# Slot tiles of a routed layer: probabilities folded into the rows, one operation for ReLU and sum, two of three tiles transposed by DMA, gathers five tiles ahead

## The chip, the core and the metric

The kernel runs on one core of one Trainium2 chip. The metric is device time in microseconds (us), the median of several executions. The core has five engines with their own instruction queues: TensorE (PE in the profile), VectorE (DVE), ScalarE (ACT), GpSimd (POOL) and SyncE (SP). SP here only issues DMAs; POOL also issues the indirect ones.

## The reference, cut to what matters

Two layers run over 4096 tokens of 512 features. The first (attention to a context, then a quantised feed-forward net) and the attention of the second lie before everything that is changed here. The change is in the last part, a net of eight experts that takes the best expert for each token:

```
probs = softmax(x @ Wg + bg)
idx   = argmax(probs)
p     = probs[idx]
e     = idx % 8
out   = relu(x @ We[e] + be[e]) * p      # for the token's own expert only
x     = x + out                          # x in the product is the layer norm of x
```

Here `x` in the products is the normalised row, `x` in the last line the row itself.

## The kernel before

**Tiles.** Tokens lie in 32 tiles of 128 rows. For the experts they are sorted by expert into 39 slot tiles, each of which holds rows of one expert. This sorting is done twice. The first, `routing(True)`, runs along with the attention of tiles 24 to 28 and fills slot tiles 0 to 14 (`NJA = 15`) from the first 22 tiles. The second, `routing(False)`, is cut into steps that stand between `expert(5)` and `expert(11)` and fills slot tiles 15 to 38. Its last steps build one-hot tables on DVE (L1134), and PE multiplies them (32 short matmuls, L1142) to find out which row goes where. DVE then turns the product into row numbers (L1144 to L1148).

**A row in memory.** For each tile `gated` (L996 to L1009) writes to `x_dram` rows of 516 numbers: the 512 of x, the mean, the reciprocal deviation, the probability p and a zero.

**A slot tile.** For slot tile j the work is this. `gathered(j)` (L1159): POOL issues an indirect DMA that brings 128 rows into `xw[j % 6]`. `centered_x(j)` (L104): DVE takes the mean away and multiplies by the reciprocal deviation. `turned_x2(j)` transposes the tile, in one of two ways that `by_dma(j)` picks. Either PE transposes four blocks (L116) and ACT takes them from PSUM, adding 4.0 (`RAISE`) in the first partition (L1185). Or DVE adds RAISE to four columns (L1171) and splits the floats into halves of 16 bits (L826), SP issues a transposing DMA (L829), and ACT joins the halves (L832). The first five tiles and then every even one go by PE, the odd ones from 5 on by DMA. `expert(j)` then has PE multiply by the expert's matrix (L1195), ACT take ReLU of p times the product (L1198), DVE add x (L1199), and POOL scatter the rows to the output by another indirect DMA (L1200). RAISE carries the expert's bias: a row of the weights was prepared so that the raised feature brings it in.

**Order.** From the second layer on, PE, DVE, ACT and POOL run in the order in which the program is written. `expert(j)` issues in this order: gather j+4, transposition of j+1, the matmuls of j, centering of j+3, ReLU and sum of j, scatter of j. So on DVE the centering of j+3 stands ahead of the sum of j, and on POOL the gather of j+4 stands ahead of the scatter of j. Each scatter writes the same output tensor and waits until the one before it has landed. Four PSUM buffers (`psm`) serve products and transpositions.

**Where it starts.** When the first sorting is done, in the pass of tile 28, gathers 0 to 3 are issued. In the pass of tile 29 slot tiles 0 to 2 are centered and tile 0 is transposed. `expert(0)` and `expert(1)` stand in the passes of tiles 30 and 31, and `expert(2)` to `expert(4)` among the last steps of these. From `expert(5)` on nothing is left but slot tiles and the second sorting.

Of the kernel before, what the change touches and what calls it, by code (L numbers as in the profile page):

```python
# [16 lines left out]
U16 = mybir.dt.uint16  # L17
I8 = mybir.dt.int8
AF = mybir.ActivationFunctionType
ALU = mybir.AluOpType  # L20
# [4 lines left out]
P = 128  # L25
B, S, T, D = 2, 2048, 128, 512
ND = D // P
# [16 lines left out]
NJA = NTA - (NE - 1)  # L44
# [4 lines left out]
RAISE = 4.0  # L49
# [14 lines left out]
def two_layers(ctx: ExitStack, tc: tile.TileContext, a, out):  # L64
    nc = tc.nc
# [37 lines left out]
    def center(dst, x, mean, scale):  # L103
        nc.vector.tensor_scalar(dst, x, mean, scale, ALU.subtract, ALU.mult)  # L104
# [720 lines left out]
    def split(x, planes):  # L825
        nc.vector.tensor_copy(  # L826
            planes.rearrange("p (h f) -> p h f", h=2), x.bitcast(U16).rearrange("p (f h) -> p h f", h=2)
        )
        nc.sync.dma_start(out=x.bitcast(U16).rearrange("p (b q) -> p b q", q=P), in_=planes, transpose=True)  # L829

    def joined(dst, x):
        nc.scalar.copy(  # L832
            dst.bitcast(U16).rearrange("p c (q h) -> p h c q", h=2),
            x.bitcast(U16).rearrange("p (h c q) -> p h c q", h=2, c=ND),
        )
# [181 lines left out]
    def part(n, shape, dtype=F32, at=0):  # L1017

        size = math.prod(shape)
        v = xw[n][:, at : at + (size * mybir.dt.size(dtype) + 3) // 4]  # L1020
        if dtype is not F32:
            v = v.bitcast(dtype)[:, :size]
        if len(shape) == 1:
            return v
        names = "abc"[: len(shape)]
        return v.rearrange(f"p ({' '.join(names)}) -> p {' '.join(names)}", **dict(zip(names, shape)))
# [130 lines left out]
    def gathered(j):  # L1157
        if j < NJ:
# [2 lines left out]
                in_offset=bass.IndirectOffsetOnAxis(ap=tile_of[j][2], axis=0),  # L1161
            )

    def centered_x(j):
        if j < NJ:
            x = xw[j % 6]
            xn = part(6 + j % 3, [D])
            center(xn, x[:, :D], x[:, D : D + 1], x[:, D + 1 : D + 2])
            if by_dma(j):
                first = xn.rearrange("p (c q) -> p c q", c=ND)[:, :, 0:1]  # L1170
                nc.vector.tensor_scalar(first, first, RAISE, None, ALU.add)  # L1171
                split(xn, part(24 + j // 2 % 2, [2 * D], U16))

    def by_dma(j):

        return j > 4 and j % 2 == 1

    def turned_x2(j):
        if j < NJ and by_dma(j):
            ring[j] = part(9 + j % 3, [ND, P])  # L1180
            joined(ring[j], part(6 + j % 3, [D]))
        elif j < NJ:
            pt = transposed(psm, part(6 + j % 3, [D]))
            ring[j] = part(9 + j % 3, [ND, P])
            nc.scalar.activation(ring[j], pt, AF.Identity, bias=raised)  # L1185

    def expert(j):

        te, tok, _ = tile_of[j]
        gathered(j + 4)  # L1190
        turned_x2(j + 1)
        e = nc.tensor.value_load(te, min_val=0, max_val=NE - 1)
        pz = psm.tile([P, D], F32, name="pz", tag="m")
        for c in range(ND):
            nc.tensor.matmul(pz, ring[j][:, c, :], we[:, bass.ds(e, 1), c, :], start=(c == 0), stop=(c == ND - 1))  # L1195
        centered_x(j + 3)
        x, acc = xw[j % 6], part(12 + j % 3, [D])
        nc.scalar.activation(acc, pz, AF.Relu, scale=x[:, D + 2 : D + 3])  # L1198
        nc.vector.tensor_tensor(acc, acc, x[:, :D], ALU.add)  # L1199
        nc.gpsimd.indirect_dma_start(  # L1200
            out=out_rows, out_offset=bass.IndirectOffsetOnAxis(ap=tok, axis=0),
            in_=acc, in_offset=None, bounds_check=NT * P - 1, oob_is_err=False,
        )
# [32 lines left out]
    for n in range(NT):  # L1236
        blk, t = n // NB1, n % NB1
        ahead = blk + 1 < nblk
        fs = range(t * ND // NB1, (t + 1) * ND // NB1)
        if n > 0:  # L1240
            biased(n - 1)
        firsts = [m for m in (n + 2 * NB1, n + 2 * NB1 + 1) if m < NT and (m >= TURNED) == (m > n + 2 * NB1)]
        firsts = [normed(m) for m in firsts]
        scores(n)
        if 4 <= n < 4 + 2 * NE and n % 2 == 0:

            nc.scalar.dma_start(out=rowadd, in_=v_dram[(n - 4) // 2].partition_broadcast(P))

        late = t == 0 and n > 1
        if ahead and not late:  # L1250
            queries(blk + 1, fs[:1])
        if late:
            logits(n - 2)
        exponentials(n)
        if ahead and late:
            queries(blk + 1, fs[:1])
        if n == 0:
            for i in range(NT - held, NT - held + 2):
                down(i)
# [12 lines left out]
        if n + 1 < NT:  # L1272
            kept_keys(n + 1)
        for first in firsts:
            if first:
                first()
        if 0 < n <= NE:
            load(we[:, n - 1], a["L1_ffn_We"][n - 1].rearrange("(c p) f -> p c f", p=P))
        if ahead:
            queries(blk + 1, fs[1:])  # L1280
        if n == 0:
            for i in range(NT - held + 2, NT):
                down(i)
            dwn.close()
            ffd.close()
            moe = ctx.enter_context(tc.tile_pool(name="moe", bufs=1, side="right"))
            we = moe.tile([P, NE, ND, D], F32, name="we")
        if 4 <= n < 4 + 2 * NE:
            e, half = divmod(n - 4, 2)
            for c in range(2 * half, 2 * half + 2):  # L1290
                nc.gpsimd.tensor_tensor(we[:, e, c, :], we[:, e, c, :], rowadd, ALU.add)
        if not ahead:

            expert(n - NT + NB1)
        turned(n)
        if rest:
            rest()
        if n > 0:
            turned2(n - 1)
        mixed(n)  # L1300
        if t == NB1 - 1 and blk + 2 < nblk:
            for t in range(NB1):
                turned1((blk + 2) * NB1 + t)
        if n == NTA + 2:
            route = routing(True)
        if route:
            for _ in range({NTA + 2: 4, NTA + 3: 1}.get(n, 2)):
                if next(route, route) is route:
                    route = None
                    for j in range(4):  # L1310
                        gathered(j)
                    break
        if n == NT - NB1 - 1:
            for j in range(3):
                centered_x(j)
            turned_x2(0)
    biased(NT - 1)
# [58 lines left out]
```

## Time and profile before

| | us |
|---|---|
| median of 3 runs | 1600.61 (1597.93, 1601.0, 1600.61) |
| the profiled execution's own time | 1599.43 |
| its span in the profile | 1597.4 |
| PE busy in the span | 1551.3 (97%) |
| DVE busy | 1192.5 (75%) |
| expert(0) on PE | from 1408.78 |
| expert(5) on PE | from 1455.70 |
| one-hot products of the second sorting | 1477.28 to 1480.61 |
| expert(11) to expert(38) on PE | 1481.32 to 1587.39 |
| last scatter issued | 1589.12 |

Times in a timeline count from the start of the span. A line of a timeline gives start, duration, engine, line of the kernel, operation, tiles written and read, and in brackets the idle time of the engine before it with what ended it. A line of the groups gives busy time and mean nanoseconds of one instruction. "Landing" is the time from the issue of a DMA to its completion.

### The profile page before, as it was taken

To read this page: it belongs to the slowest core of one execution; us is meant where nothing else is said; L and a number is where in the kernel's file an instruction comes from. 1 tells how busy PE (TensorE), PEld (TensorE's weight loads), DVE (VectorE), ACT (ScalarE), POOL (GpSimd) and SP (SyncE) were. 2 spreads that over 40 slices of the span, in tenths; PEclk is the share of its full clock that TensorE was granted. 3 is DMA by queue.
4 is the path that set the end of the run, shared out by engine and by line. 5 is a ranking of instruction groups with operands and counts; after the bars stand their busy time and mean duration, and the time that the engine had idled before them with its cause. 6 is when DMAs were issued, how large, how long until landed. Compare 5 with 4: busy or idle time off the path is not lost. (4 is left out here: it accounts for less than half of the span.)

```text
span 1597.4 us, 26167 instructions
## 1 busy us (share of the span) xinstructions
PE 1551.3 (97%) x9542; PEld 909.1 (57%) x9542; DVE 1192.5 (75%) x2333; ACT 720.4 (45%) x1537; POOL 586.8 (37%) x580
## 2 busy tenths in 40 slices
PE   7999999999999999999999999999999999999997
PEld 5655555555555555544444466666666666654443
DVE  3467777777777886589986678888888888877442
ACT  1222222222222222243335566777777776763442
POOL 2232222222222222110005654555565444544553
PEclk9999999999999999999999999999999999999999
DMA  9511212111111220367768734221311111114553
GB/s 321 188 37 41 47 40 47 40 47 40 51 46 41 59 60 1 117 169 205 179 173 278 271 132 143 48 47 34 55 45 36 41 28 41 41 47 131 162 162 89
DMA packets 180571, 150.90 MB, mean 94 GB/s; under 512 B 97089, under 2 KB 144665, under 8 KB 180444
## 3 DMA queue, kind: packets, MB, share of 16 engines
q1 hardware_dynamic: 170188, 127.25, 28.5%
q0 software_dynamic: 6240, 18.70, 3.8%
q10 hardware_dynamic: 4016, 3.29, 0.9%
q8 instruction: 76, 1.25, 0.3%
q14 instruction: 51, 0.42, 0.1%
HBM read 89.97 MB, written 41.79 MB: 82 GB/s over the span
## 5 line engine op out<-in xcount | busy, mean ns | idle before, releaser
L419 ACT ACTIVATE pr<-sc 128x1024 f32<-128x1024 f32 x64 | 65.6, 1024 | 421.6 <-PE sc L414 421.4
L393 PE MATMUL pq<-xnT,wq 128*128 128x256 f32 x1024 | 254.4, 391 | 0.0
L451 PE MATMUL pw<-wo,att 128*128 128x512 f32 x512 | 230.8, 593 | 0.0
L393 PEld LDWEIGHTS pq<-xnT,wq 128*128 128x128 f32 x1024 | 184.4, 189 | 67.1 <-issue 44.0
L914 ACT ACTIVATE s<-s,mx 128x128 f32<-128x128 f32 x512 | 175.3, 388 | 28.1 <-DVE mx L905 28.1
L923 POOL TENSOR_TENSOR s<-s,rs 128x1024 f32<-128x1024 f32 x64 | 120.9, 1903 | 149.6 <-DVE rs L922 149.1
L403 POOL TENSOR_TENSOR q<-rt,rt 128x256 f32<-128x256 f32 x64 | 46.7, 730 | 339.7 <-DVE rt L402 335.2
L451 PEld LDWEIGHTS pw<-wo,att 128*128 128x128 f32 x512 | 96.9, 190 | 96.4 <-issue 89.9
L441 DVE RECIPROCAL rd<-sc 128x256 f32<-128x256 f32 x64 | 112.4, 1757 | 46.5 <-PE sc L435 46.5
L1195 PE MATMUL pz<-we,x 128*128 x312 | 139.3, 598 | 1.8 <-ACT x L832 1.6
L872 PE MATMUL pq<-xT,wq 128*128 128x256 f32 x512 | 122.6, 382 | 0.0
L978 PE MATMUL pl<-wgate,xnT 128*128 128x512 f32 x256 | 116.7, 599 | 0.0
L955 PE MATMUL pw<-wo,oT 128*128 128x512 f32 x256 | 115.2, 592 | 0.7 <-ACT oT L946 0.7
L872 PEld LDWEIGHTS pq<-xT,wq 128*128 128x128 f32 x512 | 96.0, 190 | 33.1 <-issue 20.3
L398 DVE TENSOR_TENSOR rt<-pq,rope_cos 128x256 f32<-128x256 f32 x64 | 27.0, 422 | 104.2 <-PE pq L393 104.2
L749 ACT ACTIVATE gate<-pg,gsc 128x512 f32<-128x512 f32 x88 | 60.5, 687 | 93.9 <-PE pg L744 84.0
L1195 PEld LDWEIGHTS pz<-we,x 128*128 128x128 f32 x312 | 58.2, 192 | 68.4 <-issue 65.2
L92 DVE BATCH_NORM_STATS2 st<-x 128x6 f32<-128x512 f32 x130 | 89.4, 688 | 6.0 <-DMA x<-in_ctx 3.8
L744 PE MATMUL pu<-xqT,wuT 128*128 128x512 bf16 x352 | 90.3, 379 | 2.6 <-DVE h L752 2.4
L744 PE MATMUL pg<-xqT,wgT 128*128 128x512 bf16 x352 | 90.3, 379 | 0.0
L900 DVE SCALAR_TENSOR_TENSOR s<-sc,keep 128x1024 f32<-128x1024 f32 x64 | 78.1, 1220 | 14.3 <-PE sc L892 9.1
L955 PEld LDWEIGHTS pw<-wo,oT 128*128 128x128 f32 x256 | 48.6, 190 | 55.3 <-issue 53.6
(226 smaller groups left out, 2811.8 us busy)
## 6 DMA issues: line engine op xcount, KB each, us to landing
h_dram<-h SPq DMA_DIRECT2D x88, 256.0 KB
hq<-h_dram SPq DMA_DIRECT2D x31, 704.0 KB
x_dram<-x SPq DMA_DIRECT2D x32, 258.0 KB
x<-in_x SPq DMA_DIRECT2D x32, 256.0 KB
we<-in_L_ffn_We SPq DMA_DIRECT2D x8, 1024.0 KB
xnT<-in_x_turned SPq DMA_DIRECT2D x14, 512.0 KB
along<-stat_dram SPq DMA_DIRECT2D x14, 256.0 KB
w_in<-in_L_ffn_w_gate SPq DMA_DIRECT2D x11, 256.0 KB
```

Of the source, the lines that this page charges most:

```text
L92: nc.vector.bn_stats(out=st, in_=x)
L393: nc.tensor.matmul(pq, wqs[c // 2][:, c % 2, par, g * P : (g + 1) * P], xnTs[k][:, c, :], start=(c == 0), stop=(c == ND - 1))
L441: nc.vector.reciprocal(rd, sc[:, 0, B0:])
L451: nc.tensor.matmul(pw, atts[u][:, f, t * P : (t + 1) * P], wo[:, 2 * g + f, :], start=(g == 0 and f == 0), stop=(g == NG - 1 and f == 1),)
L744: nc.tensor.matmul(dst, w[:, c, i * P : (i + 1) * P], xqTs[blk][:, c, :], start=(c == 0), stop=(c == ND - 1),)
L872: nc.tensor.matmul(pq, wq1[:, c, f * P : (f + 1) * P], xTs[blk][:, c, :], start=(c == 0), stop=(c == ND - 1))
L900: nc.vector.scalar_tensor_tensor(s, sc[:, 2 * half : 2 * half + 2].rearrange("p r c k -> p (r c) k"), -MASKED, keeps[n].unsqueeze(1).to_br ...
L914: nc.scalar.activation(s[:, h, :], s[:, h, :], AF.Exp, bias=mx[:, h : h + 1], **accum)
L923: nc.gpsimd.tensor_tensor(s, s, rs.unsqueeze(2).to_broadcast([P, 8, T]), ALU.mult)
L955: nc.tensor.matmul(pw, os_[n][:, c, :], wo1[:, c, :], start=(c == 0), stop=(c == ND - 1))
L978: nc.tensor.matmul(pl, xn2T[n][:, c, :], wgate[:, c, :], start=(c == 0), stop=(c == ND - 1))
L1195: nc.tensor.matmul(pz, ring[j][:, c, :], we[:, bass.ds(e, 1), c, :], start=(c == 0), stop=(c == ND - 1))
```

## The change

Five edits to the slot tiles:

1. **p goes into the rows.** DVE multiplies the reciprocal deviation by p first (one number per row, kept in column 515 of the row), and centering multiplies by that. RAISE must be multiplied by p as well: DVE adds p times RAISE to the four columns of every tile, whichever way it is transposed. ACT's copy out of PSUM no longer adds anything.
2. **ReLU and sum are one DVE operation** from PSUM: the larger of product and zero, plus x. ACT's ReLU is gone, and the sum stands ahead of the centering in DVE's order.
3. **Two of three tiles are transposed by DMA**: from 5 on those whose number 3 does not divide. 23 tiles go this way, where it was 17, and 16 by PE, where it was 22. The buffers for the halves alternate by j % 2.
4. **Gathers are five tiles ahead, centering four**, each one more than before. Five gathers and four centerings stand at the start, where it was four and three. The centered tiles get a fourth buffer, the room of tile 26.
5. **At the second sorting** tiles 15 and 16 can't be gathered before it is done. expert(10) issues no gather, expert(11) issues both and centers nothing, expert(12) centers both.

```diff
+    def xn_of(j):
+        return part((6, 7, 8, 26)[j % 4], [D])
     def centered_x(j):
         if j < NJ:
-            x = xw[j % 6]
-            xn = part(6 + j % 3, [D])
-            center(xn, x[:, :D], x[:, D : D + 1], x[:, D + 1 : D + 2])
+            x, xn = xw[j % 6], xn_of(j)
+            p = x[:, D + 2 : D + 3]
+            rp = x[:, D + 3 : D + 4]
+            nc.vector.tensor_tensor(rp, x[:, D + 1 : D + 2], p, ALU.mult)
+            center(xn, x[:, :D], x[:, D : D + 1], rp)
+            first = xn.rearrange("p (c q) -> p c q", c=ND)[:, :, 0]
+            nc.vector.scalar_tensor_tensor(first, p.to_broadcast([P, ND]), RAISE, first, ALU.mult, ALU.add)
             if by_dma(j):
-                first = xn.rearrange("p (c q) -> p c q", c=ND)[:, :, 0:1]
-                nc.vector.tensor_scalar(first, first, RAISE, None, ALU.add)
-                split(xn, part(24 + j // 2 % 2, [2 * D], U16))
+                split(xn, part(24 + j % 2, [2 * D], U16))
     def by_dma(j):
-        return j > 4 and j % 2 == 1
+        return j > 4 and j % 3 > 0
     def turned_x2(j):
...
-            nc.scalar.activation(ring[j], pt, AF.Identity, bias=raised)
+                nc.scalar.copy(ring[j], transposed(psm, xn_of(j)))
     def expert(j):
         te, tok, _ = tile_of[j]
-        gathered(j + 4)
+        for i in () if j == NJA - 5 else (NJA, NJA + 1) if j == NJA - 4 else (j + 5,):
+            gathered(i)
         turned_x2(j + 1)
...
-        centered_x(j + 3)
         x, acc = xw[j % 6], part(12 + j % 3, [D])
-        nc.scalar.activation(acc, pz, AF.Relu, scale=x[:, D + 2 : D + 3])
-        nc.vector.tensor_tensor(acc, acc, x[:, :D], ALU.add)
+        nc.vector.scalar_tensor_tensor(acc, pz, 0.0, x[:, :D], ALU.max, ALU.add)
+        if j != NJA - 4:
+            for i in (NJA, NJA + 1) if j == NJA - 3 else (j + 4,):
+                centered_x(i)
...
-                    for j in range(4):
+                    for j in range(5):
                         gathered(j)
...
-            for j in range(3):
+            for j in range(4):
                 centered_x(j)
```

More of the change, by code (lines that the diff above doesn't have):

```diff
@@ L1162, in gathered @@
             )
+    def xn_of(j):
+        return part((6, 7, 8, 26)[j % 4], [D])
     def centered_x(j):
         if j < NJ:
-            x = xw[j % 6]
-            xn = part(6 + j % 3, [D])
-            center(xn, x[:, :D], x[:, D : D + 1], x[:, D + 1 : D + 2])
+            x, xn = xw[j % 6], xn_of(j)
[5 more added lines that the diff above has]
+            nc.vector.scalar_tensor_tensor(first, p.to_broadcast([P, ND]), RAISE, first, ALU.mult, ALU.add)
             if by_dma(j):
-                first = xn.rearrange("p (c q) -> p c q", c=ND)[:, :, 0:1]
-                nc.vector.tensor_scalar(first, first, RAISE, None, ALU.add)
-                split(xn, part(24 + j // 2 % 2, [2 * D], U16))
+                split(xn, part(24 + j % 2, [2 * D], U16))
     def by_dma(j):
-        return j > 4 and j % 2 == 1
+        return j > 4 and j % 3 > 0
     def turned_x2(j):
-        if j < NJ and by_dma(j):
+        if j < NJ:
             ring[j] = part(9 + j % 3, [ND, P])
[L1181 to L1185, printed above, removed]
+            if by_dma(j):
+                joined(ring[j], xn_of(j))
+            else:
+                nc.scalar.copy(ring[j], transposed(psm, xn_of(j)))
     def expert(j):
         te, tok, _ = tile_of[j]
-        gathered(j + 4)
+        for i in () if j == NJA - 5 else (NJA, NJA + 1) if j == NJA - 4 else (j + 5,):
+            gathered(i)
         turned_x2(j + 1)
```

## The prediction

> **What bounds the kernel now.** I read the page first: PE is busy almost throughout.
>
> ```profile
> PE 1551.3 (97%) x9542; PEld 909.1 (57%) x9542; DVE 1192.5 (75%) x2333; ACT 720.4 (45%) x1537; POOL 586.8 (37%) x580
> ```
>
> So an edit counts if it takes work from PE's order or ends a PE stall. Next, PE's timeline over the slot tiles, to set its work against the clock:
>
> ```profile
> 1477.28 0.57 PE L1142 MATMUL pid<-x,x 128*128 128x48 bf16 x16
> 1478.97 0.37 PE L1142 MATMUL pid<-x,x 128*128 128x48 bf16 x8 [1.13 <-DVE x L1134]
> 1480.11 0.50 PE L1142 MATMUL pid<-x,x 128*128 128x48 bf16 x8 [0.76 <-DVE x L1134]
> 1480.44 1.09 PE L116 MATMUL pt<-ident,x 128*128 128x128 f32 x4
> 1481.32 8.10 PE L1195 MATMUL pz<-we,x 128*128 x16
> 1489.26 0.60 PE L116 MATMUL pt<-ident,x 128*128 128x128 f32 x4
> 1489.70 7.03 PE L1195 MATMUL pz<-we,x 128*128 x16
> 1580.26 7.13 PE L1195 MATMUL pz<-we,x 128*128 x16 [0.75 <-ACT x L832]
> ```
>
> One expert takes 3.43 us start to start (1447.80 to 1451.23), a PE transposition 0.44 (1489.26 to 1489.70), a pair of tiles with one transposition 7.30. From 1489.70 to 1580.26 are 12 pairs, 90.56 us; their work is 87.6, so PE stalls 3.0 us there, most of it late, for ACT's join (L832). Earlier PE waits for DVE's one-hot tables: the second sorting is bound by DVE. What that costs besides, the windows show (length; busy time of PE, PEld, DVE, ACT, POOL; granted clock; DMA share; GB/s):
>
> ```profile
> 1477.00:1480.40 3.40, 1.51 (x34) 1.01 (x32) 3.05 (x4) 1.89 (x2) 2.38 (x2) 0.95 0.45 155
> 1480.40:1484.00 3.60, 3.60 (x14) 2.13 (x11) 2.76 (x8) 0.69 (x1) 2.13 (x3) 0.57 0.43 124
> 1484.00:1490.00 6.00, 6.00 (x18) 2.86 (x17) 2.78 (x5) 2.46 (x3) 3.44 (x4) 1.00 0.63 188
> ```
>
> After the wait the clock is 0.57 for 3.6 us: 1.55 us lost. Last, why joins are late. POOL's timeline:
>
> ```profile
> 1541.18 1.02 POOL L1200 DMA_INDIRECT out_x<-x,x  x1 [1.67 <-DMA out_x<-x,x]
> 1542.51 1.05 POOL L1159 DMA_INDIRECT x<-x_dram,x  x1 [0.30 <-ACT x L1185]
> 1544.72 1.02 POOL L1200 DMA_INDIRECT out_x<-x,x  x1 [1.16 <-DVE x L1199]
> 1548.44 1.02 POOL L1200 DMA_INDIRECT out_x<-x,x  x1 [1.42 <-DMA out_x<-x,x]
> ```
>
> A scatter waits for the landing of the last one, and the gather behind it waits too. Issue to issue is landing plus 0.8 us: 2.7 and 3.54 for the first scatter here. Landings, scatter by scatter, from 1498.88 to 1575.32: 2.6 to 3.0 (mean 2.7) in slots without a transposing DMA, 2.9 to 4.0 (mean 3.3) with one, 2.1 in the last four with neither gather nor transposition. The gather's landing (median 3.7) then holds DVE, whose centering stands ahead of the sum that the next scatter needs. This loop over two tiles takes about 7.6 us against PE's 7.30, and 75.95 us for the 20 tiles from 1504.31 to 1580.26 is 3.80 a tile.
>
> **The change part by part**, against the profiled execution (1599.43; span 1597.4).
>
> *Fewer PE transpositions.* After the one-hot products PE transposes tiles 12, 15, ..., 36, nine instead of the fourteen even ones: 5 x 0.44 = -2.2. The one saved before (6 and 9 instead of 6, 8 and 10) is covered by the wait for DVE.
>
> *The loop.* The sum of j no longer waits for gather j+3 behind it in DVE's order; in its place DVE waits there for PE's product, with the centering of j+4 and the next sorting step queued behind. A gather issued after scatter j-1 now serves tile j+5, one tile (3.6 us) later. From the end of expert(j-4): sum 0.75 after 0.2 (nearest row: L752, a STT from PSUM, 743 ns), 0.2 + 0.57 + 0.2 for the three small steps, split 0.69, transposing DMA 3.6 to 4.6 (from the end of L826 to the start of L832, 1521.24 to 1524.84 and 1512.74 to 1517.32), join 1.34: 7.6 to 8.6 us, and PE needs it after three tiles, 10.7. Stalls gone: -3.0, with 0.3 left for collisions. Bounds 0 and -3.0. On POOL the gather of j+5 has to wait for the sum of j-1, whose room it fills, and scatter j is queued behind; but scatter j-1 just ahead waits for the same sum, so this adds nothing.
>
> *The last tile.* ACT 0.69 and DVE 0.69 after the product (1587.43 to 1588.84, 1.41) become one DVE operation, 0.74: -0.67. Elsewhere the removed ReLU is off the path, save in the passes of tiles 30 and 31 (below).
>
> *DVE in the second sorting.* From L1199 of tile 5 (1460.15) to the last L1134 (ends 1480.05) DVE never idles: 19.9 us, of which sorting steps 13.2, five sums at 0.60 and centerings of 9 to 12 (1.38 with a split, 0.46 without). After: five sums at 0.67 = 3.35; five centerings, 9 to 13, three with split at 0.2 + 0.57 + 0.2 + 0.6 = 1.57 and two without at 0.93 = 6.57; steps 13.2; together 23.1. The small ones are priced by L1171 (0.17, and 0.20 to the next). Without ACT's 0.7 us ahead the first sum starts that much sooner. 23.1 - 19.9 - 0.75 = +2.45, all on the path, since PE's products, their row numbers and expert(11) come after. Bounds +1.7 (small steps at 0.1) to +3.2.
>
> *The clock.* PE's wait grows from 2.3 us with a batch in it to about 5 (expert(10) ends near 1477). The row says half speed for about 3.1 us after it, 1.55 lost. I take +0.2, bounds -1.55 (no loss) to +1.55 (twice the row).
>
> The Trainium skill ("TensorE: Matmul & The Clock Gate", Part 1) states a free-running window of 3413 ns: one idle window halves the clock, one busy window restores it. By it the loss depends on where the windows fall, an estimate of 1.7 instead of 1.55, which the trace's 3.1 us at half speed agrees with; it speaks against lengthening this wait.
>
> *The start.* A fifth gather puts 0.95 + 0.30 = 1.25 us on POOL ahead of `biased` (L949, 1390.46) and the shares (L923, which had 0.62 spare at 1392.37), and so on L101, L821 and PE's transposition at 1397.91: about +0.45. In the pass of tile 29 DVE centers four tiles, not three (2.40 us at 1398.40): one more (0.54) and eight small steps, together 2.2, less the 0.76 idle before L900 at 1401.57. With the 0.45, L900 and its chain through exponentials, shares, L101 and L821 come 1.9 later; PE's transposition at 1413.96 has 0.3 spare after L821: +1.6 in all. Back comes this: ACT's ReLU stood ahead of its copies L931, and PE's mixing (L941) took 1.66 in these two passes against 1.30 before, -0.7. Net +0.9, bounds -0.7 to +1.7.
>
> *Transpositions by DMA.* 23 instead of 17, six more DMAs on SP, where almost only transpositions are queued by then. That of tile 5 moves ahead of the row write of tile 29 (some 1.3 us); these rows are first read at 1484.79, so that is covered. ACT has 1.34 x 2/3 + 0.6/3 = 1.1 us a tile, under PE's 3.58. What they do to scatters is the first rival.
>
> Sum: -2.2 - 3.0 + 0.3 - 0.67 + 2.45 + 0.2 + 0.9 = -2.0. The profiled execution lies 1.2 under the median; the mean of all four times shown is 1599.75, and 1599.75 - 2.0 = 1597.7. I say 1598.0, leaning a little to the first rival.
>
> **The rivals.**
>
> *A. The chain of scatters decides.* Before, scatter(11) is issued at 1487.72; by the terms above it is then near 1490.6. 23 intervals x follow that hold a gather, then four without one at 2.88 (1580.09 to 1582.97), 11.5 us. At x = 3.70 it ends where the sum does; above that it sets the end. By the landings above, two tiles in three at 3.3 + 0.8 and one at 2.7 + 0.8 make 3.9: the last issue at 1490.6 + 89.7 + 11.5 = 1591.8, 2.7 later than 1589.12, so 1602.4. At 4.0 it is 1604.7. It is slower by over 0.2% from 3.96 on. For it: landings of 3.7 and 4.0 are there late. Against: the sum now comes before the split, so a scatter can be through before its slot's transposition starts. I give 3.70 to 3.96 a chance of 0.18 (about 1601.5), and 3.96 up 0.14 (1604.7).
>
> The Trainium skill ("DMA: Bandwidth & Descriptors", Issuing engines are not separate DMA queues) states that DMAs from all issuing engines share the same 16 DMA engines and interleave; that would make six more transpositions lengthen scatters, as the landings with and without one show.
>
> *B. Start and clock cost nothing.* Without +0.9, +0.2 and 0.3, and with the clock full (-1.55): -5.0, 1594.8. For it: the chains at the start have idle time I may have undercounted. Chance 0.2.
>
> *C. The change doesn't end the stalls*, because joins are late for another reason (transposing DMAs in pairs): +1.0, 1600.7. Chance 0.08.
>
> **How the numbers follow.** My forecast has 0.40. About 0.2%, 3.2 us, is what a measurement of this kernel can tell from no change. Faster by more (under 1597.4): 0.16 from the forecast's own lower part and 0.19 of B, 0.35. Slower by more (over 1603.8): A's 0.14 and 0.05 from its lower part and from bounds that meet, 0.19. Within: 0.46. The range reaches from B (1594.6) into A (1603.2) and leaves out the worst of A and the best of B. The likeliest case alone spans 1596 to 1600.
>
> **What would show it.** Right: PE's pairs give way to triples of 10.74 us with no wait for L832; the last L1134 ends some 2.5 us later after the start's shift; a window at half clock follows; PE's mixing in the passes of tiles 30 and 31 takes 1.3; the last scatter follows the last product by 1.1 us. Wrong: scatters released by the landing of the one before in most tiles, falling further and further behind PE, or PE waits for L832 as before.

## The result, and the profile after

The changed kernel takes 1605.99 us (median of 6 runs, 1605.35 to 1608.68); the kernel before, beside it on the same chip, 1599.27 (6 runs, 1597.64 to 1601.09). The ratio is 1.0044 (95% interval 1.0034 to 1.0055): slower by 6.7 us. The forecast of 1598.0 was wrong, and the time lies above its range. The profiled execution took 1608.68 (span 1607.0), the slowest of the six, so a sum of its parts comes out some 3 us larger than the difference of the medians.

The page's first part for the changed kernel (engine, busy us, share, instructions) shows PE with 3.2 us less to do than before, in a longer span:

```profile
PE 1548.1 (96%) x9494; PEld 904.9 (56%) x9518; DVE 1207.0 (75%) x2400; ACT 699.1 (44%) x1498; POOL 583.3 (36%) x580
```

PE's timeline, at the end of the second sorting and from tile 26 on:

```profile
1485.42 0.50 PE L1142 MATMUL pid<-x,x 128*128 128x48 bf16 x8 [2.94 <-DVE x L1134]
1486.56 0.50 PE L1142 MATMUL pid<-x,x 128*128 128x48 bf16 x8 [0.63 <-DVE x L1134]
1486.88 1.09 PE L116 MATMUL pt<-ident,x 128*128 128x128 f32 x4
1487.77 11.94 PE L1202 MATMUL pz<-we,x 128*128 x24
...
1543.58 7.13 PE L1202 MATMUL pz<-we,x 128*128 x16 [0.39 <-ACT x L832]
...
1586.12 7.49 PE L1202 MATMUL pz<-we,x 128*128 x16 [0.83 <-ACT x L832]
```

expert(11) starts at 1487.77 instead of 1481.32; the wait for DVE's last tables is 2.94 us where it was 1.13. From tile 26 on PE waits for joins again. The windows around the one-hot products (columns as in the prediction):

```profile
1481.20:1486.50 5.30, 1.16 (x25) 0.81 (x23) 5.20 (x9) 0.63 (x1) 1.99 (x2) 0.76 0.52 142
1486.50:1490.80 4.30, 4.24 (x16) 2.57 (x17) 2.77 (x10) 1.82 (x2) 2.00 (x2) 0.51 0.44 116
1490.80:1496.80 6.00, 6.00 (x15) 2.66 (x14) 1.18 (x2) 1.34 (x1) 2.96 (x3) 1.00 0.56 154
```

PE is busy for 1.16 of the 5.30 us while DVE is busy throughout, and then runs 4.30 us at half clock. The trace has the half clock from 1483.90 to 1490.73: 6.83 us, where before it was 3.41. Last, POOL's timeline in the middle and at the end:

```profile
1530.56 1.02 POOL L1208 DMA_INDIRECT out_x<-x,x  x1 [2.08 <-DMA out_x<-x,x]
1531.88 1.24 POOL L1159 DMA_INDIRECT x<-x_dram,x  x1 [0.30 <-issue]
1535.99 1.02 POOL L1208 DMA_INDIRECT out_x<-x,x  x1 [2.88 <-DMA out_x<-x,x]
...
1589.84 0.98 POOL L1208 DMA_INDIRECT out_x<-x,x  x1 [2.80 <-DMA out_x<-x,x]
1592.70 0.98 POOL L1208 DMA_INDIRECT out_x<-x,x  x1 [1.87 <-issue]
1595.57 0.98 POOL L1208 DMA_INDIRECT out_x<-x,x  x1 [1.89 <-DMA out_x<-x,x]
1598.41 0.98 POOL L1208 DMA_INDIRECT out_x<-x,x  x1 [1.86 <-issue]
```

A scatter here is issued when the one before has landed, not when its rows are ready. The last product ends at 1593.61 and the last scatter is issued 4.8 us later (1.7 before).

I cut each profile at four points: the output projection (L955) of tile 28's pass near 1390 (the parts ahead of it vary from execution to execution and are left out), the start of expert(5), scatter(11), scatter(34).

| us | before | after | difference |
|---|---|---|---|
| L955 near 1390 to expert(5) | 64.97 | 69.04 | +4.1 |
| expert(5) to scatter(11) | 32.02 | 33.84 | +1.8 |
| scatter(11) to scatter(34), 23 intervals | 87.60 (3.81 each) | 92.19 (4.01) | +4.6 |
| scatter(34) to the last one | 13.80 | 12.37 | -1.4 |

So the loss has three places: the start, the second sorting, and the chain of scatters. The experiments ask what makes each. These times are of one execution of each kernel, and they scatter from execution to execution; where that matters it is said below.

### The profile page after: what moved, and what is told of

Read it like the earlier page. It is cut to its first block, busy times and chain, and to the rows that moved or that the text cites. A ratio compares the mean times of both kernels' runs of the same rounds, so it can differ in the third digit from the quotient of the medians.

```text
span 1607.0 us, 26085 instructions
## 1 busy us (share of the span) xinstructions
PE 1548.1 (96%) x9494; PEld 904.9 (56%) x9518; DVE 1207.0 (75%) x2400; ACT 699.1 (44%) x1498; POOL 583.3 (36%) x580
## 5 line engine op out<-in xcount | busy, mean ns | idle before, releaser
L914 ACT ACTIVATE s<-s,mx 128x128 f32<-128x128 f32 x512 | 175.3, 388 | 29.6 <-DVE mx L905 29.6
L978 PE MATMUL pl<-wgate,xnT 128*128 128x512 f32 x256 | 116.7, 599 | 0.0
L955 PE MATMUL pw<-wo,oT 128*128 128x512 f32 x256 | 115.2, 593 | 1.3 <-ACT oT L946 1.3
L810 PE MATMUL py<-wdT,hb 128*128 128x512 bf16 x343 | 77.0, 379 | 3.7 <-DVE hb L804 2.5
```

Source lines behind the costliest of these rows:

```text
L914: nc.scalar.activation(s[:, h, :], s[:, h, :], AF.Exp, bias=mx[:, h : h + 1], **accum)
L955: nc.tensor.matmul(pw, os_[n][:, c, :], wo1[:, c, :], start=(c == 0), stop=(c == ND - 1))
L978: nc.tensor.matmul(pl, xn2T[n][:, c, :], wgate[:, c, :], start=(c == 0), stop=(c == ND - 1))
```

## The experiments

All against the kernel before on the same chip. The ratio compares medians. The other columns are the first three rows of the table above, in us, taken from each kernel's own profile, which is one execution; it lies between 2.9 us under its kernel's median (f1, g2) and 3.9 over it (e3).

| kernel | ratio (95% interval) | to expert(5) | to scatter(11) | mean interval |
|---|---|---|---|---|
| e1 change, two scatter targets | 1.0011 (1.0002 to 1.0020) | 69.0 | 33.5 | 3.63 |
| e2 before, two scatter targets | 0.9985 (0.9974 to 0.9996) | 66.2 | 31.0 | 3.75 |
| e3 change, ReLU on ACT for 0 and 1 | 1.0047 (1.0033 to 1.0060) | 69.9 | 33.3 | 3.99 |
| e4 change, every odd tile by DMA | 1.0046 (1.0032 to 1.0060) | 69.0 | 34.2 | 4.11 |
| f1 change, gathers four ahead | 1.0076 (1.0063 to 1.0089) | 69.3 | 37.0 | 3.93 |
| f2 before, edits 4 and 5 alone | 1.0021 (1.0010 to 1.0031) | 65.8 | 34.0 | 3.99 |
| f3 before, one of three by DMA | 0.9986 (0.9977 to 0.9996) | 66.4 | 30.6 | 3.82 |
| f4 change, start as before | 1.0053 (1.0041 to 1.0066) | 70.1 | 35.1 | 3.90 |
| g1 before, edit 1 alone | 1.0015 (1.0006 to 1.0023) | 66.5 | 33.9 | 3.95 |
| g2 before, edits 1 and 2 alone | 1.0026 (1.0013 to 1.0039) | 68.7 | 31.7 | 3.87 |
| g3 before, edit 3 alone | 1.0025 (1.0014 to 1.0036) | 66.2 | 31.6 | 4.01 |
| g4 before, DMA only from tile 15 | 0.9997 (0.9989 to 1.0006) | 66.6 | 30.5 | 3.98 |
| h1 change, no transposing DMA | 1.0024 (1.0014 to 1.0033) | 68.5 | 29.6 | 3.91 |
| h2 change, one of three by DMA | 1.0035 (1.0025 to 1.0045) | 68.5 | 31.1 | 4.04 |
| h3 before, no transposing DMA | 1.0004 (0.9995 to 1.0013) | 65.3 | 29.8 | 3.87 |

**Does the chain of scatters carry the loss?** In e1 and e2 odd tiles scatter to a scratch tensor, so two chains run side by side (their rows don't reach the output).

```diff
+    out_b = dram.tile([NT * P, D], F32, name="out_b")
-            out=out_rows, out_offset=...
+            out=out_rows if j % 2 == 0 else out_b, out_offset=...
```

> The changed kernel, but the scatters of odd slot tiles go to a scratch tensor of the output's size, so that their rows don't reach the output; each scatter then waits for the one two before it. Theory (the chain of scatters sets the end): in the changed kernel the 23 intervals from scatter(11) to scatter(34) take 4.01 us each and the last scatter comes 4.8 us after the last product. With two chains the gathers come on time, PE's stalls for L832 from tile 26 on (4.2 us) go, and the last scatter follows the last product by 1.1 us: 4.2 + 3.7 = 7.9 us less than 1606.0, about 1598. Rival (joins are late because transposing DMAs come in pairs): the stalls stay and only the lag at the end goes, 3.7 less, 1602.3. Rival (the end is PE's, delayed at the start and in the second sorting): under 1 us less.

> The kernel before, with the scatters of odd slot tiles to the same scratch tensor (their rows don't reach the output). If the chain of scatters was what held PE back there too, its 3.0 us of stalls after 1489.70 go: 1596.3 against 1599.3. If not, 1599.3. Together with the changed kernel with two targets it prices the rest of the change without the chain: by the theory that kernel is then still slower by 1 to 2 us (start +4.1, second sorting +2.1, clock +0.5; fewer transpositions -2.2, last tile -0.7, and 3.0 of stalls gone in both).

The change gains 0.33 points, about 5.3 us where 7.9 were expected, and the kernel before 0.15, about 2.4. In e1 nearly every interval is PE's own pace (3.43, and 3.87 with a PE transposition), and the last scatter follows the last product by 1.0 us. Waits of the change from 1490 to 1600, and of e1 from 1494 to 1592 (who waited for whom: us in total, times, longest):

```profile
DVE x L1173 <- DMA x<-x_dram,x: 31.8, 21, 2.6
...
POOL out_x L1208 <- DMA out_x<-x,x: 18.9, 10, 2.9
...
PE pz L1202 <- ACT x L832: 2.6, 5, 0.8
```

```profile
DVE x L1174 <- DMA x<-x_dram,x: 5.9, 5, 1.7
...
POOL out_x L1209 <- DMA out_b<-x,x: 2.2, 2, 1.5
...
PE pz L1203 <- ACT x L832: 0.8, 2, 0.5
```

With two chains DVE hardly waits for gathered rows any more and PE hardly for joins. So the chain costs the change some 3 us more than it costs the kernel before (the intervals of the ratios allow 0 to 6). What is left between e1 and e2, 0.26 points or 4.2 us, has nothing to do with the chain. In their profiles the start has 2.8 us of it and the second sorting 2.5, and 1.4 come back later.

**The start.** PE's timeline shows three waits there that it did not have before:

```profile
1400.99 0.63 PE L116 MATMUL pt<-ident,x 128*128 128x128 f32 x4 [0.95 <-DVE x L1173]
...
1416.38 0.66 PE L116 MATMUL pt<-ident,s 128*128 128x128 f32 x4 [1.41 <-DVE x L1204]
...
1433.18 0.66 PE L116 MATMUL pt<-ident,s 128*128 128x128 f32 x4 [0.81 <-DVE x L1204]
```

The first waits for centering with its small operations. The other two are the fourth transposition of the shares in the passes of tiles 30 and 31. It needs a PSUM buffer, and of the four three hold earlier transpositions and one holds expert(0)'s or expert(1)'s product. Before, ACT's ReLU emptied that one at once; now it is held until DVE comes to its sum. The single edits price these (lines that are only taken away are left out here):

```diff
 g1 (edit 1 alone, in the kernel before)
+            nc.vector.tensor_tensor(rp, x[:, D + 1 : D + 2], p, ALU.mult)
+            nc.vector.scalar_tensor_tensor(first, p.to_broadcast([P, ND]), RAISE, first, ALU.mult, ALU.add)
 g2 = g1 and
-        nc.scalar.activation(acc, pz, AF.Relu)
-        nc.vector.tensor_tensor(acc, acc, x[:, :D], ALU.add)
+        nc.vector.scalar_tensor_tensor(acc, pz, 0.0, x[:, :D], ALU.max, ALU.add)
```

> The kernel before with the first edit alone: p multiplied into the reciprocal deviation, p times RAISE added to every tile; ReLU stays on ACT (without the scale) and the sum a DVE operation of its own. Theory (the small operations are on the path where DVE is): in the pass of tile 29 PE waits for them ahead of the transposition of tile 0 (0.95 us in the change), at the start about 1.3 us in all; in the second sorting four tiles get 0.2 each for p and two of them 0.2 for RAISE, 1.2. Chain of scatters as before (3.81), begins 2.5 later: ratio 1.0015. Rival (the idle time of DVE covers them): ratio 1.000.

> The kernel before with the first two edits alone: p in the rows, ReLU and sum one DVE operation from PSUM (after the centering, as the sum was before). Theory: on top of the first edit's 2.5 us, the product's PSUM buffer is held until DVE's late sum, so the fourth transposition of the shares waits in the passes of tiles 30 and 31 (1.4 and 0.8 us in the change), +2; back come 0.7 in the second sorting, where DVE no longer waits for ACT, and 0.67 at the last tile. Ratio 1.002. Rival, as the prediction had it (no PSUM wait, PE's mixing shorter by 0.7): less than the first edit alone, ratio 1.0005.

PE's timeline of g1 has the wait for the small operations, that of g2 the wait for the buffer (here just before the mixing, L941, because the centering still stands ahead of the sum):

```profile
1400.63 0.63 PE L116 MATMUL pt<-ident,x 128*128 128x128 f32 x4 [0.73 <-DVE x L1170]
```

```profile
1414.07 1.08 PE L941 MATMUL po<-s,v 128*32 128x128 f32 x32 [0.81 <-DVE x L1201]
...
1430.64 1.08 PE L941 MATMUL po<-s,v 128*32 128x128 f32 x32 [0.65 <-DVE x L1201]
...
1457.24 7.10 PE L1198 MATMUL pz<-we,x 128*128 x16 [0.83 <-DVE x L1201]
```

By these waits edit 1 costs 0.73 us (0.95 in the change), and edit 2 costs 2.3 (the last of its three waits is ahead of expert(5)), where the change has 1.41 and 0.81. f2, which has the fifth gather and the fourth centering without either edit, has no new wait of PE over 0.35. The whole times to expert(5), 66.5 in g1, 68.7 in g2 and 65.8 in f2 against 65.0, are no sharper than 1.2 us: g3, which does the same work as the kernel before up to expert(5), has 66.2, and what it has more is idle time of PE ahead of L955 (1.90 us instead of 0.68; more on it below). The change has 0.65 more of this idle time too; without that its 4.07 are 3.4.

In the second sorting the time from expert(5) to the end of the last L1134 on DVE is the better measure: 24.36 us before and 24.35 in e2, 26.49 in the change and 26.39 in e1. It is 25.64 in g1, 24.89 in g2, 24.30 in g3 and 25.92 in f2. So edit 1 costs 1.28 us, edit 2 gives 0.75 back, edit 3 does nothing (-0.06), and edits 4 and 5 cost 1.56; together 2.03, where the change lost 2.13.

Two attempts to mend the start in the change failed:

```diff
 e3
+        if j < 2:
+            nc.scalar.activation(acc, pz, AF.Relu)
+            nc.vector.tensor_tensor(acc, acc, x[:, :D], ALU.add)
 f4: at the start range(4) gathers and range(3) centerings; expert(0) gathers 4 and 5, centers 3 and 4
```

> The changed kernel, but in expert(0) and expert(1) ACT takes ReLU of the product and DVE adds x, as before. Theory (PSUM): in the passes of tiles 30 and 31 the fourth transposition of the shares waits for the PSUM buffer of the expert's product, which DVE frees late in its order (PE waits of 1.41 and 0.81 us for L1204). With ACT freeing it these two waits go, and the 0.65 us more that PE waits for oT; 2.2 to 2.9 us less, expert(5) on PE at about 1457.4 instead of 1460.0, and as everything after shifts alike, 1603.1 to 1603.8. Rival (the start is late because of DVE's fourth centering and its small steps): the waits are taken over by the shares or by xn, expert(5) at 1459 to 1460, under 1 us less.

> The change with the start as before: four gathers in the pass of tile 28 and three centerings in that of tile 29; the fifth gather and the fourth centering move into expert(0), which so issues gathers 4 and 5 and centers 3 and 4. Theory: of the 4.1 us that the change loses up to expert(5), the fifth gather is 0.5 and the fourth centering with the small operations about 1 to 1.5 in the pass of tile 29; the waits for PSUM buffers (1.41 and 0.81 us) stay. expert(5) starts 1.5 us earlier, the chain of scatters 1.5 us earlier too, and so the end: ratio 1.0035. Rival: the two centerings in expert(0) lie on DVE's way to the shares of the next pass and take it back: ratio 1.0044 as before.

In e3 the two waits are gone, and PE's transpositions and mixing follow each other without a gap. But in the pass of tile 31 ACT's copy of the mixed values (L946) started 1.9 us after the mixing had ended (0.7 in the change), and after PE's idle time there (2.55 us) the record has 3.41 us of half clock: its next step took 5.24 us instead of 3.70. So that the two waits cost the whole kernel their 2.2 us is read from PE's timeline; the run that takes them away does not show it.

```profile
1438.57 5.24 PE L955 MATMUL pw<-wo,oT 128*128 128x512 f32 x8 [2.55 <-ACT oT L946]
```

Why that copy is late is open. The idle time before this step is 0.7 us in before, f2, h1, h2 and h3, 0.8 in g1, 1.2 to 1.3 in the change, e1, e4, f1 and f4, and 1.8 to 1.9 in e2, f3, g2, g3 and g4, without a reason that the profile names. In f4 the waits became 0.96 and 1.64, and nothing was gained, as its rival said: the two centerings in expert(0) lie on the same way.

**What makes a scatter slow: the number of transpositions, their time, or something else?** First, fewer of them, and gathers four ahead:

```diff
 e4:  -        return j > 4 and j % 3 > 0      +        return j > 4 and j % 2 == 1
 h2:  -        return j > 4 and j % 3 > 0      +        return j > 4 and j % 3 == 1
 f1:  -        for i in () if j == NJA - 5 else (NJA, NJA + 1) if j == NJA - 4 else (j + 5,):
      +        for i in (j + 4,):              (and centered_x(j + 4) without exceptions; four gathers at the start)
```

(e4 also takes the buffers of the halves by `j // 2 % 2`, as the kernel before does.)

> The changed kernel with every odd tile from 5 on transposed by DMA, as before (17, not 23), all else kept. Theory (chain): an interval between scatters is 4.1 us with a transposing DMA in the slot and 3.5 without, so 23 of them shrink from 4.01 to 3.8 us each: 4.6 to 4.8 less, and with fewer splits in the second sorting about 1600.5 to 1601.5, although PE transposes five more tiles (+2.2), which lie beside the chain. Rival (the chain doesn't matter, PE's order does): 2.2 us more, 1608, less what the stalls for L832 give back (at most 4.2).

> The change with one of three tiles transposed by DMA (7, 10, ..., 37; eleven instead of twenty-three). Theory (number and time of meetings): intervals 3.57 x 2/3 + 4.0 to 4.3 x 1/3 = 3.71 to 3.8, 23 of them 85 to 87.5 instead of 92.2; PE's order 3.72 a tile; two splits less in the second sorting, -1.6. Together -5 to -7 us at S(34), less what the last four give back: ratio 1.001 to 1.002. Rival (as with every odd tile by DMA, where nothing came back although there were six transpositions less): 1.004.

> The change with the fourth and fifth edits undone in part: gathers four tiles ahead as before (four at the start, no exception at the second sorting), centering of j+4 still behind the sum of j. Theory (phase): what lengthens a scatter is not how many transpositions there are but when they start. With gathers four ahead the centering waits for a gather issued 1.3 us after a scatter, so the transposition starts at a fixed 2.5 us after a scatter (1.0 before the next) as in the kernel before; with five ahead it follows PE and drifts into the scatters' packets. So: intervals of about 4.0 with and 3.57 without a transposition, mean 3.86 instead of 4.01, 23 of them 3.4 us shorter; the fifth gather gone from the start another 0.5. Ratio about 1.0044 - 0.0024 = 1.002, 1603 where the kernel before has 1600. Rival (number): 23 transpositions instead of 17 make the chain 4.0 whatever their time; ratio 1.004, only the 0.5 us of the start comes back.

Neither number helped: 4.11 us an interval with 17 transposing DMAs, 4.04 with 11, and ratios of 1.0046 and 1.0035, over what was expected. So the simple theory (each costs 0.44) fell. f1, which was to keep their time, failed too: its ratio is 1.0076 where 1.002 was expected, and its intervals are 3.93. In h2 intervals without one are 3.56 on average, those with one 4.3 to 5.9 (in three of these eight a block of instructions passed as well, of which more below). POOL's and SP's timelines of h2 show the worst meeting, a transposition issued 0.07 us after a scatter:

```profile
1578.01 1.02 POOL L1208 DMA_INDIRECT out_x<-x,x  x1 [1.26 <-DVE x L826]
1583.78 1.00 POOL L1208 DMA_INDIRECT out_x<-x,x  x1 [4.75 <-DVE x L1204]
```

```profile
1578.08 1.23 SPq L829 DMA_TRANSPOSE x<-x  x1
```

Its packets ended 4.49 us after the issue. (The releaser in the brackets is the last event seen; sum and split were long done.) Now take all transposing DMAs away:

```diff
-        return j > 4 and j % 3 > 0
+        return False
```

> The change with every tile transposed by PE (no transposing DMA, no split, no join; all other edits kept). Theory: the intervals between scatters are long because transpositions meet scatters. Without any they fall to the 3.57 us of slots without one, and PE's order decides: 3.87 us a tile, 23 of them 89 us instead of the 92.2 between scatters before; DVE has three splits less in the second sorting (2.4 us). Last scatter 1.1 us behind the last product. Ratio 1.002 to 1.003, and intervals of 3.87 everywhere. Rival (scatters are slow for another reason, gathers or loading of code): intervals stay at 4.0, only the 2.4 us of the second sorting come back, and scatters lag behind PE as before.

> The kernel before with every tile transposed by PE. Theory: the chain of scatters is then off the path and PE's order alone decides: 28 tiles from expert(11) on at 3.87 are 108.3 us where they took 106.1 (with 3.0 of stalls and 1.55 of clock), the second sorting ends about 1.5 us sooner and the clock stays whole: together -0.5 to +1 us, ratio 0.9995 to 1.0005; intervals of scatters 3.87. Rival (scatters slow for another reason): intervals of 3.8 to 4.0 with long ones among them, stalls for late rows, ratio 1.001 to 1.002.

Both went as the theory said. POOL's timeline of h1:

```profile
1506.22 1.26 POOL L1208 DMA_INDIRECT out_x<-x,x  x1 [1.33 <-DVE x L1173]
...
1510.09 1.26 POOL L1208 DMA_INDIRECT out_x<-x,x  x1 [1.33 <-DVE x L1173]
...
1515.11 1.02 POOL L1208 DMA_INDIRECT out_x<-x,x  x1 [2.48 <-DVE x L1176]
...
1518.50 1.02 POOL L1208 DMA_INDIRECT out_x<-x,x  x1 [1.09 <-DVE x L1176]
```

Scatters come every 3.87 us, with PE. Three of 23 intervals are longer (5.02 from 1510.09 to 1515.11, 5.10, 4.65) and are made up by shorter ones. In each of the three a packet of 16 KB of the instruction queue passed while the scatter's packets were under way (1511.41, 1542.94 and 1573.38, 0.9 to 1.4 us each). h1 against h3, run together, is 1602.88 to 1599.61: 3.3 us, and their traces differ by 3.2 us up to expert(5). With no transposing DMA the chain is off the path, and what the rest of the change still costs is the start.

To see time and number apart I put together the 345 intervals of the fifteen profiles with one target (before, after, and all kernels but e1 and e2), by when a transposing DMA was issued and whether a block of instructions passed. A block is one large packet of an instruction queue; it counts where it is under way between 1.0 us after the scatter's issue and the scatter's last packet. Without anything else a scatter's last packet is 2.39 us after its issue, and the next scatter mostly follows 1.2 to 1.3 after that packet.

| transposition issued, against the scatter | scatters | last packet after issue, mean (most) |
|---|---|---|
| none | 162 | 2.39 (2.75) |
| 2.2 to 1.5 us before | 17 | 2.93 (3.92) |
| 1.5 to 1.0 before | 31 | 2.59 (3.08) |
| 1.0 to 0.6 before | 58 | 2.85 (3.45) |
| 0.6 to 0.2 before | 17 | 3.15 (3.37) |
| 0.2 before to 0.6 after | 6 | 3.97 (4.49) |
| 0.6 to 1.9 after | 11 | 2.46 (2.85) |
| none, but a block of instructions | 22 | 2.97 (4.28) |
| both | 20 | 3.42 (4.59) |

(One scatter met two transpositions and is left out.) So by this grouping the time counts, more than the number. The first of the rows with a transposition does not fit the rise that follows it: at that distance the transposition should be nearly through, and why some of these scatters were long is open. In the change the transposition starts some 1.6 us after the sum (two small operations, centering, split), and the scatter follows the sum at once if the chain is in time, or later by what it has fallen behind. Falling behind by 1 to 2 us would put the scatter on top of the transposition; in the change's own profile the nearest is issued 0.31 us before its scatter. This reading of the intervals is put together afterwards; the runs without transposing DMAs show the part with or without one, the phases are a grouping, not an experiment. The Trainium skill ("DMA: Bandwidth & Descriptors", Queues, rings and completion order) states that each DMA engine goes round its queues packet by packet. That would put a large packet of another queue ahead of a scatter's; blocks of 8 and 16 KB that take up to 1.7 us, beside scatters 0.6 us longer on average, agree, but no run here shows the order on an engine.

The blocks also say how little the mean interval of one profile tells. Without the intervals that met one it is 3.80 us in the kernel before (21 intervals), 3.86 in the change (19), 3.84 in f2, 3.87 in h2, 3.90 in f1 and 3.98 in e4 and g3. The change's other four, with a block, have 4.72 on average (two in the kernel before have 3.94). So of the 4.6 us that the change's profile loses from scatter(11) to scatter(34), some 3 stand where blocks met scatters in this one execution. What the chain costs is told by e1, e2 and h1, which compare medians, and not by this column.

**The other edits alone, in the kernel before.**

```diff
 f2:  -        gathered(j + 4)    +        for i in () if j == NJA - 5 else (NJA, NJA + 1) if j == NJA - 4 else (j + 5,): gathered(i)
      (centered_x(j + 4) behind the sum, xn_of(j), five gathers and four centerings at the start)
 g3:  -        return j > 4 and j % 2 == 1    +        return j > 4 and j % 3 > 0      (and the halves by j % 2)
```

> The kernel before with the fourth and fifth edits alone: gathers five ahead, centering of j+4 behind the sum of j, four centered buffers, the exceptions at the second sorting. Same transpositions (every odd tile by DMA), p and ReLU as before. Theory (phase): the transposition no longer follows a gather, it drifts into scatters' packets; intervals 3.81 -> 4.0 to 4.1 as in the change with every odd tile by DMA (4.11 there), 23 of them +4.4 to +6.9, start +1.5 from the fifth gather and fourth centering: ratio 1.0035 to 1.005, as slow as the whole change or nearly. Rival (number, small operations): the loop loses its stalls (-3) and pays the start (+1.5): ratio 0.999 to 1.001.

> The kernel before with the third edit alone: two of three tiles from 5 on transposed by DMA. Theory (a meeting of transposition and scatter costs 0.44, and gathers four ahead keep them from the worst meetings): intervals 2/3 x 4.0 + 1/3 x 3.57 = 3.86 instead of 3.81, 23 of them +1.1; one more split among the tiles of the second sorting, +0.9; PE's order is 2.2 shorter but not what decides. Ratio 1.001. Rival A (number alone makes the chain 4.0): +4.4 and +0.9, ratio 1.003. Rival B (PE's order decides): ratio 0.9985.

f2's ratio is 1.0021, between what theory and rival said. Its intervals are as the theory said (3.99), but that profile is the slowest of its eight executions, and without the intervals with blocks they are 3.84; so this is no support for the phase. g3 came out near the rival that only counts: 4.01 and +0.25%. Each part alone is slower than nothing: +0.26% (edits 1 and 2), +0.25% (3), +0.21% (4 and 5), together +0.72%, where the whole is +0.44%. So the parts don't simply add, and f1 shows one place where they help each other. Its waits from 1458 to 1490:

```profile
PE pid L1142 <- DVE x L1134: 6.6, 4, 3.1
...
DVE x L1173 <- DMA x<-x_dram,x: 4.4, 4, 2.4
```

With gathers four ahead DVE waits 4.4 us for rows in the second sorting; in the whole change that wait is not there, and PE's wait is 4.2. expert(5) to scatter(11) is 37.0 in f1 and 33.8 in the change: with the added DVE work there and the centering of j+4 kept, the fifth gather ahead is worth 3.2 us. (In f1 gather and centering of j+4 stand in the same expert(j), so the rows have less time to come than in either kernel.)

**A version that beats both.** One of three or none of the early tiles by DMA, in the kernel before:

```diff
 f3:  -        return j > 4 and j % 2 == 1    +        return j > 4 and j % 3 == 1     (and the halves by j % 2)
 g4:  -        return j > 4 and j % 2 == 1    +        return j > 14 and j % 2 == 1
```

> The kernel before with one of three tiles transposed by DMA instead of one of two (7, 10, ..., 37; eleven instead of seventeen), else as it was. Theory: every meeting of a transposition and a scatter costs 0.44 us of the chain; 23 intervals go from 3.81 to 3.57 x 2/3 + 4.0 x 1/3 = 3.71, -2.3 us; PE does 0.44 more for one tile in six, +1.7 in its order, but had 3.0 us of stalls there; the splits of tiles 9 and 11 leave DVE's second sorting and that of 10 comes: -0.6. Together -1 to -2.3 us, ratio 0.9985 to 0.9995. Rival (number doesn't matter, PE's order decides): +1.7 us, ratio 1.001.

> The kernel before with no transposition by DMA before tile 15 and every odd one from 15 on: the splits of tiles 5 to 13 leave DVE's second sorting. Theory: with one of three by DMA the second sorting ended 1.4 us sooner and PE kept its full clock; without any split there DVE is about 2 us sooner, PE has five transpositions more in front (2.2 us) where it waited 2.3 us for DVE; the clock's 1.55 us stays in hand, the chain of scatters has 3.81 as before. -1.5 to -3 us, ratio 0.998 to 0.999. Rival (PE's five transpositions move the one-hot products as much as DVE gains): ratio 1.000.

f3 is the fastest that keeps the whole computation: 1598.36 us against 1600.79, ratio 0.9986, a gain of 0.14% (0.04 to 0.23). The gain is not where I expected it: the mean interval is 3.82, as before. From expert(5) to scatter(11) it is 1.4 us shorter, with no half-clock stretch behind the one-hot products, and the last four scatters are 1.15 quicker. g4 missed its forecast: with the same short second sorting its ratio is 0.9997, no change that could be told. Its intervals are 3.98, though from tile 15 on it is written as the kernel before; why the same pattern gives 3.81 once and 3.98 once is open. A single profile's mean interval is no better than that.

## Why the prediction was wrong, step by step

- **PE's transpositions (-2.2).** The work did go: 3.2 us less PE busy. But it was booked at full price on a path that the scatters set.
- **The loop (-3.0 + 0.3).** This is one of the two steps that failed. PE has no bracket for L832 from 1499.98 to 1542.59, as the working said. Then rows come late, since DVE waits for gathers that stand behind late scatters. PE's time from expert(11) on is 105.84 us, of which 28 x 3.43 + 9 x 0.44 = 100.0 is work and some 2 the clock, so about 4 us of stalls are left, where 0.3 was booked. The step compared the loop with PE's pace and did not run the chain beside it, though its own reading had 3.80 us a tile where PE needs 3.65. With two chains (e1) PE waits 0.8 us for joins, and the change gains 5.3: the step's sum for PE's own loop holds, and what it left out is the chain. (The 3.43 us of one expert were read from the product at 1447.80, which is the router's, L978; the pairs of tiles give 3.43 as well.)
- **The last tile (-0.67).** Nothing: the last scatter waits for the one before it, not for its sum. Where the chain doesn't hold it the term is there: the last scatter follows the last product by 1.01 us in e1 and h1, by 1.73 in e2 and h3.
- **DVE in the second sorting (+2.45).** The last L1134 ends 6.45 us later, of which 4.3 come with expert(5): 2.1. Right, and the single edits add up to it: 1.28 for the small operations (g1), 0.75 back without ACT's ReLU (g2), just what the step had, and 1.56 with the centering one further ahead (f2).
- **The clock (+0.2).** The half-clock stretch is twice as long in the records; part of it falls on idle PE, and PE loses about 2.1 instead of 1.55. Small, and in part luck: e1, e3 and f4, with nearly the same waits (2.94 or 2.98 us, then 0.76), have 3.41 us of half clock, and e2, with the waits of the kernel before, has none. The length of the window that the prediction cited from the Trainium skill ("TensorE: Matmul & The Clock Gate", Part 1) agrees: 6.83 us are two windows of 3413 ns. But the window ahead of the drop was not idle; PE was busy for 40% of it, and for 46% in the kernel before (the last section has more).
- **The start (+0.9, bounds -0.7 to 1.7).** This term failed most plainly: 4.1 in the profile, and 3.2 between h1 and h3, which have the same idle time ahead of L955. The fifth gather and fourth centering, which the step priced, cost at most 0.8 (f2). The small operations made PE's first transposition wait 0.73 to 0.95. And the wait for the PSUM buffer, 2.2 in the change, was not in the working at all: the step counted removing ReLU from ACT as a gain (-0.7, "ACT's ReLU stood ahead of its copies") and did not ask who else waits for what ReLU releases. The four buffers and their users were in the code.
- **Rival A.** It had the mechanism: 4.0 an interval, scatters that lag ever further behind PE. Its start, scatter(11) at 1490.6, was 3.3 early (1493.85), by the start's error. Its 3.9, from landings "with" and "without" a transposition, is near the 3.86 of the intervals without a block; blocks of instructions, which make the rest of the profile's 4.01, were in no term. Its weight was too low, and "the sum now comes before the split, so a scatter can be through before" is true only of a scatter in time. The outcome that came had been given 0.14.
- **Rivals B and C** did not happen: the start costs more, not less, and joins are late through the chain.

## What to carry to other kernels

Before an operation is taken off an engine because it has time, list what that operation releases (here a PSUM buffer) and who takes it next: the engine that inherits the release may come much later. Where transfers wait for each other in a chain, make the sum for the chain as for an engine, from its own first link, and ask what else will pass while a link of it is under way. Don't take a difference of a few us from one profile of each kernel: look at the same stretch in a run whose program is the same there. And price small operations where the engine has no idle time; here two of 0.15 to 0.17 us a tile cost 0.15% in a kernel of 1600 us.

## What the runs showed of the hardware that was not expected

- A block of the instruction queues (one packet of 16 KB, 0.9 to 1.7 us, or of 8 KB, mostly 0.3 to 0.7 us) that passes while a scatter is under way lengthens it: the last packet at 2.97 instead of 2.39 us on average, 4.28 at most. In this part of the program one of 16 KB comes some 30 us after the other.
- A transposing DMA within 0.2 us before to 0.6 after a scatter's issue makes it longest, 3.97 us to the last packet (six scatters); one issued 0.6 to 1.9 after hardly touches it (2.46).
- After the waits of 2.94 and 0.63 us with a short batch between them the half clock lasted 6.83 us in the records, twice that of the kernel before; in f1, after 2.19, 0.63, 3.11 and 0.63, it lasted 10.24, three times. Full and half clock change at the ends of windows of 3.413 us, counted on from any such change of the same trace. In the seventeen traces, from 60 to 1592 us, 29 windows at full clock were followed by one at half, and PE was busy for at most 48% of each; no window under 42% was followed by full clock, and none over 48% by half. At half clock PE had to be busy for more of a window: up to 76% it stayed, from 92% on full clock came back.
